# A hybrid of selective scan, convolution and spectral layers: one C multiply of twelve moves from GpSimd to VectorE, softplus's PSUM bank is counted as free one slot later, and one bias of three in the feed-forwards moves to VectorE

## The chip, the cores and the metric

The kernel runs on one core of a Trainium2 chip. The metric is the device time of one launch in microseconds, and lower is better. The engines are named as in the profile: PE is TensorE (matmuls; PEld are its weight loads), DVE is VectorE, ACT is ScalarE, POOL is GpSimd, SP is SyncE, whose queue issues all the DMAs here.

## The reference, cut to what matters

The input is x, four images of 96 channels and 64 by 64 pixels. Each goes through a group norm and four layers:

```python
# layer 0, a selective scan; K = 4 directions, DI = 192 channels, N = 16 states, L = 4096 pixels
u = silu(depthwise_conv3x3(Win @ x) + conv_b)
xs = [u, transposed u, reversed u, reversed transposed u]
dts_r, Bs, Cs = split(sel_w[k] @ xs[k])                  # 6, 16 and 16 rows
delta = softplus(dt_w[k] @ dts_r + dt_b)
for l in range(L):                                       # for each direction, channel d, state n
    h[d, n] = h[d, n] * exp(delta[d, l] * A[d, n]) + delta[d, l] * xs[d, l] * Bs[n, l]
    y[d, l] = sum_n h[d, n] * Cs[n, l]
y = layer_norm(sum of the four directions + Ds * xs); x = x + Wout @ y

# layer 1: 1x1 expansion to 576, depthwise 3x3, 1x1 back, with batch norms and relu
# layer 2: a spectral layer (FFT over the 4096 pixels, relu(X * r + b), inverse FFT), then a feed-forward
# layer 3: linear attention with 6 heads, then a feed-forward
# both feed-forwards, on layer-normed tokens, 96 -> 384 -> 96, with the rounding of fp8e5 and fp16:
h = relu(fp16(fp16(fp8(x) @ fp8(W1).T) + fp8(b1)))
y = fp16(fp16(fp8(h) @ fp8(W2).T) + fp8(b2))
```

## The kernel before, in words

**The scan.** The scan runs over 128 steps: 4 images, 4 directions each, 8 chunks of 512 pixels each. A step has 12 units; a unit is 64 channels (two halves `e` of 32) by 4 states, so 128 partitions by two times 512 elements. Four engines work on a unit, each in the order in which the instructions are written:

- GpSimd multiplies the step's delta times u (`rep_g`) with B (`rep_BC`): one product of 128x1024, `db`, in `inputs` (line 1206).
- ScalarE computes exp(delta times A) into a PSUM bank, `ps_da`, once for each half, in `decays` (line 1216). There are four such banks, which is two units.
- VectorE runs the recurrence with TENSOR_TENSOR_SCAN, once for each half, in `states` (line 1225).
- The result is multiplied with C. The units listed in `POOL_C` write the scan's result to SBUF (`hc`), and GpSimd multiplies both halves in one instruction, in `product` (line 1244). For the others the scan writes over `ps_da`, and VectorE multiplies each half into `hc` (line 1229).
- The last column of a unit's states is kept for the next chunk (`keep`): by GpSimd for the units of `POOL_C` (line 1241, one copy for both halves), by ScalarE for the others (line 1239, a copy for each half). The last chunk of a direction keeps nothing.
- PE sums over states and channels into the bank `ps_y`, for two units at a time, in `sums` (line 1265).

The scan is one loop over slots, one for each of the 1536 units. In slot s it writes out, in this order: the DMAs due; the state copies of unit s - 1 and the exponentials of unit s + 1; the C product of unit s - 1, if it is GpSimd's; the product db of unit s + 2; the scans of unit s; the sums of the pair that ended two slots ago. `db` and `hc` have three and five buffers.

**The work beside it.** All the rest (the inputs of the scan of later images, called fronts; the re-ordering of the directions, called turns; the convolutions; the spectral layers; layers 2 and 3) is cut into small portions on PE, ScalarE and VectorE, written as Python generators. A planner writes portions into each slot behind the scan's instructions. A portion states its engine, an assumed time, and the number of banks `mm` that it takes: `yield ac(0.65)` is one of 0.65 us on ScalarE. A slot has an allowance of 3.0 us on PE, 2.4 on ScalarE and 1.5 on VectorE. A stream's next portion on another engine is written in a later slot than the one before it, as a rule. There are three `mm` banks; `held_banks` counts those in use. `bank()` adds one where a matmul is written, and `free()` takes one off where the last reader of the bank is written, so that a matmul into that bank may be written in the same slot. At the start of each slot the count `freed` is taken off `held_banks` and set to zero:

```python
            tensor[0] = 0.0
            held_banks[0] -= freed[0]
            freed[0] = 0
```

Nothing adds to `freed` in the kernel before.

The stages come in the order of `plan`: weights, front 1, front 2, then for image 0 turn, convolution, spectral twice, layer 2, layer 3, then front 3, then the same for images 1 and 2, where layer 3 has the next image's turn beside it. The last image's convolution starts under the scan; when the scan is over (`alone` is filled then) the rest of it and layers 2 and 3 of the last image run without the planner.

**Softplus** (`scan_inputs`, lines 590 to 619) makes delta. A part is one matmul of the step sizes (lines 594, 598), three activations, Abs, Exp and Ln, on ScalarE (603, 605, 607), a maximum and addition on VectorE in the bank (609), the product with u (612), and a copy of the bank to SBUF on ScalarE (616). There are three parts for each of 16 chunk and direction pairs of an image. The last line of a part calls `free()`.

**The feed-forwards** (`feed_forward`) have three groups of 128 hidden rows, m = 0, 1, 2. Each is a matmul in fp8 (884), a copy to fp16 on ScalarE (887), bias and relu on ScalarE (895) or, in the part after the scan, on VectorE (892), and a conversion to fp8 (901, or 898 on VectorE for m = 1 after the scan).

Of the kernel before, what the change touches and what calls it, by code (L numbers as in the profile page):

```python
# [41 lines left out]
KORDER = [(0, 1, 3, 2)] * (B - 1) + [(1, 3, 0, 2)]  # L42

SCAN = {"rep_d": 3, "rep_g": 3, "rep_BC": 5, "db": 3, "hc": 5}
POOL_C = (1, 3, 5, 7, 9, 11)
TMP, IN = 10, 5

PC = NI * NJ // 2
# [46 lines left out]
def hybrid_kernel(ctx: ExitStack, tc: tile.TileContext, a: dict):  # L95
# [18 lines left out]
    alone = []  # L114
# [5 lines left out]
    def bank(tag="mm", turn=True):  # L120

        if alone and tag == "mm" and turn:
            tag = turns(alone)
        if tag == "mm":
            held_banks[0] += 1
        return psum.tile([128, CH], F32, name=f"ps_{tag}", tag=tag, bufs=BANKS[tag])

    held_banks, freed = [0], [0]

    def free(n=1):  # L130

        held_banks[0] -= n


    tc.keep_in_program_order(nc.scalar.preload_act_table_set("natural_log_exp_and_others"))
# [5 lines left out]
    def const(name, rows=slice(0, 128)):  # L141
        return cst[rows, CS[name]]

    def col(name, i=0, rows=slice(0, 128)):
        at = COL[name].start + i
        return cols[rows, at : at + 1]
# [40 lines left out]
    def tmp(name, shape=(128, CH), dtype=F32):  # L187

        if alone and dtype == F32:
            tag = turns(spare)  # L190
            if tag in SCAN:
                return pair(tag)[:, 0, : shape[1]]
        return bp.tile(list(shape), dtype, name=name, tag="tmp", bufs=TMP)
# [31 lines left out]
    def split(t):  # L225
        return t.rearrange("p (a b) -> p a b", a=RPC)

    def view(t, o, c):

        if o == 0:  # L230
            return split(t[:, chunk(c)])
        return t.rearrange("p (h w) -> p w h", h=H)[:, c * RPC : (c + 1) * RPC, :]
# [69 lines left out]
    def later_weights():  # L302
# [16 lines left out]
        yield dv(0.8)  # L319
        nc.vector.tensor_copy(wout_bias, p[:C, 0:1])  # L320
        free()
        nc.vector.tensor_scalar(wo_a, wo_a, col("lng_a"), None, ALU.mult)
        nc.vector.tensor_scalar(wo_b, wo_b, col("lng_b", rows=slice(0, 64)), None, ALU.mult)
# [104 lines left out]
    def later(out, t, then=None):  # L428

        to_store.append((out, t, then))  # L430
# [140 lines left out]
    def scan_inputs(b, u, o, c, done):  # L571

        i = b % 3
        if not done.issuperset([c] if o == 0 else range(NCH)):
            while not done.issuperset([c] if o == 0 else range(NCH)):
                yield wait(1)
            yield wait(2)
        ua, ub = u
        yield pe(1.8, 1)
        p = bank()  # L580
        mm(p, lhsT=sel[:, o, 0, :], rhs=view(ua, o, c), start=True, stop=False)
        mm(p, lhsT=sel[:, o, 1, :], rhs=view(ub, o, c), start=False, stop=True)

        yield ac(0.7)
        xd = tmp("xd")
        act(xd, p, AF.Identity, bias=col("one"))
        free()
        for e in (0, 1):
            later(d_bc[o + 2 * e][i][c], xd[64 * e : 64 * e + 2 * NS])
        for part in range(3):  # L590
            yield pe(0.9, 1, part > 0)
            p = bank()
            if part < 2:
                mm(p, lhsT=dtw[:, o + 2 * part, 0:128], rhs=xd, start=True, stop=True)  # L594
                at = [(slice(0, 128), o + 2 * part, slice(0, 128))]
            else:
                for e in (0, 1):
                    mm(p[64 * e : 64 * e + 64], lhsT=dtw[:, o + 2 * e, 128:DI], rhs=xd, start=True, stop=True)
                at = [(slice(64 * e, 64 * e + 64), o + 2 * e, slice(128, DI)) for e in (0, 1)]

            yield ac(0.65)
            z = tmp("z")
            act(z, p, AF.Abs)  # L603
            yield ac(0.65)
            act(z, z, AF.Exp, scale=-1.0)
            yield ac(0.65)
            act(z, z, AF.Ln, bias=1.0)  # L607
            yield dv(0.7)
            nc.vector.scalar_tensor_tensor(p, p, 0.0, z, ALU.max, ALU.add)  # L609
            yield dv(0.85)  # L610
            g = tmp("g")
            nc.vector.tensor_mul(split(g), split(p), view(ub if part == 2 else ua, o, c))
            for rows, k, ch in at:
                later(d_du[k][i][c][ch], g[rows])
            yield ac(0.6)
            nc.scalar.copy(z, p)  # L616
            free()
            for rows, k, ch in at:
                later(d_delta[k][i][c][ch], z[rows])
        traced[b].add((o, c))  # L620
# [232 lines left out]
    def layer_norm(x, out, rows=128):  # L853


        yield pe(0.9, 1)
        p = bank()
        mm(p, lhsT=const("cen", slice(0, x.shape[0])), rhs=x, start=True, stop=True)  # L858
        yield ac(0.7)
        r = tmp("r")  # L860
        act(r, p, AF.Square)
        yield pe(0.9, 1)
        v = bank()
        mm(v, lhsT=const("mean"), rhs=r, start=True, stop=True)  # L864
        yield ac(1.3)
        rsqrt(r, v)
        free()
        yield dv(0.85)
        if out.dtype == F8:
            nc.vector.tensor_tensor(out, r, p, ALU.mult, saturate=False)  # L870
        else:
            nc.vector.tensor_mul(out, split(r[:rows]), split(p[:rows]))
        free()

    def feed_forward(x, weights):

        wq1, wq2, bq = weights
        xq = tmp("xq", (128, CH), F8)
        yield from layer_norm(x[:C], xq)
        hq = tmp("hq", (128, 3, CH), F8)  # L880
        for m in range(3):
            yield pe(0.5, 1, m > 0)
            p = bank()
            mm(p, lhsT=wq1[:, m * 128 : (m + 1) * 128], rhs=xq, start=True, stop=True)
            yield ac(0.65)
            acc = tmp("acc16", (128, CH), F16)
            nc.scalar.copy(acc, p)  # L887
            free()
            if alone:

                yield dv(0.75)
                nc.vector.tensor_scalar(acc, acc, bq[:, m : m + 1], 0.0, ALU.add, ALU.max)
            else:
                yield ac(0.65)
                act(acc, acc, AF.Relu, bias=bq[:, m : m + 1])
            if alone and m == 1:
                yield dv(0.75)
                nc.vector.tensor_copy(hq[:, m, :], acc, saturate=False)
            else:
                yield ac(0.65)  # L900
                nc.scalar.activation(hq[:, m, :], acc, AF.Copy, saturate=False)  # L901
        yield pe(1.4, 1)
        p = bank()
        for m in range(3):
            mm(p[:C], lhsT=wq2[:, m, :], rhs=hq[:, m, :], start=m == 0, stop=m == 2)
        yield ac(0.65)
        acc = tmp("acc16", (128, CH), F16)
        nc.scalar.copy(acc[:C], p[:C])
        free()
        yield ac(0.65)  # L910
        act(acc[:C], acc[:C], AF.Identity, bias=bq[:C, 3:4])
        yield pe(1.4, 1)
        p = bank()
        mm(p[:C], lhsT=ident16, rhs=acc[:C], start=True, stop=False)
        mm(p[:C], lhsT=const("ident", slice(0, C))[:, :C], rhs=x[:C], start=False, stop=True)  # L915
        yield ac(0.65)
        nc.scalar.copy(x[:C], p[:C])
        free()
# [183 lines left out]
    def front(b):  # L1102


        u, there, done = [], set(), set()

        def memory():
            u.extend([big("ua")[:, :L], big("ub")[:, :L]])
            if b > 0:
                yield from normalised(b, arriving(b), there)  # L1110
                return

            chunks = [(c, fetch_image(b, c, tmp)) for c in range(NCH)]
            load(cst[:, CS["grp"]], a["cst"][:, CS["grp"]])
            load(cols, a["cols"])
            first_weights()
            yield from group_norm(b, chunks)
            yield from normalised(b, chunks, there)

        streams = [memory()]  # L1120
        for c in range(0, NCH, 2):
            streams.append(input_conv(b, u, c, there, done))
            for e in (c, c + 1):
                streams.append(scan_inputs(b, u, 0, e, done))
        streams += [scan_inputs(b, u, 1, c, done) for c in range(NCH)]
        return [Stage("front", 3 if b == 0 else 4, *streams)]
# [21 lines left out]
    def scans(stages):  # L1148
# [13 lines left out]
        for number, step in enumerate(steps):  # L1162
            step["at"] = number % (K * NCH)
            u = 0
            for which, chans in enumerate(PASSES):
                for j in range(NJ):
                    for i in chans:
                        units.append({"step": step, "number": number, "u": u, "j": j, "i": i, "pass": which,
                                      "pool": u in POOL_C})
                        u += 1  # L1170
# [402 lines left out]
```

## Time and profile before

| what | before |
|---|---|
| runs | 6701.09, 6704.47, 6705.06 us; median 6704.47 |
| profiled execution | 6709.47 us; span 6707.7 us, 84354 instructions |
| PE busy | 4872.1 us, 73% of the span |
| VectorE busy | 5391.2 us, 80% |
| ScalarE busy | 4269.2 us, 64% |
| GpSimd busy | 5488.7 us, 82% |
| granted TensorE clock, mean | 0.828 of full speed |
| HBM read and written | 881.28 and 239.01 MB, 167 GB/s over the span |

In a line of groups of the profile stand: line, engine, operation, output <- inputs (buffer numbers left out), shapes, count, then busy us and mean ns of one, then the idle time of the engine just before it and what ended most of that. A line of waits has the waiting instruction, the one that released it, the us in total, the number of times and the longest. A line of the timeline has start, us, and the instruction, with the idle time before it in brackets. In a table of stretches each engine's busy us is followed by its number of instructions.

### The profile page before, as it was taken

How to read it: one execution, taken by the hardware profiler on the slowest of the kernel's cores; microseconds unless marked ns; L12 is line 12 of the kernel's file. 1: busy time of each engine (PE TensorE's matmuls, PEld its weight loads, DVE VectorE, ACT ScalarE, POOL GpSimd, SP SyncE). 2: the span in 40 equal slices, each digit the busy share in tenths (PEclk: the TensorE clock that was granted, in tenths of full speed). 3: DMA queues.
4: the chain of work that ended last, by engine and by line, in shares of the span. 5: the costliest groups of instructions: out<-in, count | busy, mean ns of one | idle time of the engine just before them, and what ended most of it. 6: DMA issues, size and time to landing. Idle time of an engine off the chain costs nothing. (4 is left out here: it accounts for less than half of the span.)

```text
span 6707.7 us, 84354 instructions
## 1 busy us (share of the span) xinstructions
PE 4872.1 (73%) x27884; PEld 1775.4 (26%) x27884; DVE 5391.2 (80%) x5611; ACT 4269.2 (64%) x8008; POOL 5488.7 (82%) x2983
## 2 busy tenths in 40 slices
PE   7624767656987776775688877777887776859998
PEld 2101212111223521221122254211223521212383
DVE  5979888788989888888899887988988888888021
ACT  5744776654665677877466657866665676756356
POOL 4868778788999999977999988999999899899000
PEclk9756878768998887886799877878998877869998
DMA  5644555566544544455764445465644554554131
GB/s 189 197 150 144 183 189 181 174 218 219 184 148 143 199 158 147 155 186 188 246 214 146 143 160 167 157 219 186 188 147 146 189 161 161 200 180 156 35 94 38
DMA packets 438824, 1121.41 MB, mean 167 GB/s; under 512 B 73002, under 2 KB 74768, under 8 KB 437140
## 3 DMA queue, kind: packets, MB, share of 16 engines
q1 hardware_dynamic: 438388, 1116.02, 50.7%
q8 instruction: 222, 3.64, 0.2%
q14 instruction: 214, 1.75, 0.1%
HBM read 881.28 MB, written 239.01 MB: 167 GB/s over the span
## 5 line engine op out<-in xcount | busy, mean ns | idle before, releaser
L1206 POOL TENSOR_TENSOR db<-rep_g,rep_BC 128x1024 f32<-128x1024 f32 x1536 | 3602.0, 2365 | 194.1 <-DVE ps_da L1225 115.0
L1216 ACT ACTIVATE ps_da<-rep_d,aneg 128x512 f32<-128x512 f32 x3072 | 2053.5, 689 | 499.4 <-DVE hc L1225 381.7
L1225 DVE TENSOR_TENSOR_SCAN ps_da<-ps_da,state,db 128x512 f32<-128x512 f32 x1344 | 1722.9, 1282 | 371.8 <-ACT state L1239 226.7
L1244 POOL TENSOR_TENSOR hc<-hc,rep_BC 128x1024 f32<-128x1024 f32 x768 | 1813.4, 2361 | 131.8 <-DVE hc L1225 64.8
L1225 DVE TENSOR_TENSOR_SCAN hc<-ps_da,state,db 128x512 f32<-128x512 f32 x1344 | 1645.8, 1266 | 173.0 <-ACT ps_da L1216 155.9
L1265 PE MATMUL ps_y<-hc,cst 128*32 128x512 f32 x6144 | 1037.4, 755 | 781.5 <-POOL hc L1244 759.5
L1229 DVE TENSOR_TENSOR hc<-ps_da,rep_BC 128x512 f32<-128x512 f32 x1536 | 1062.3, 692 | 91.3 <-DVE ps_da L1225 1.3
L1265 PEld LDWEIGHTS ps_y<-hc,cst 128*32 128x32 f32 x6144 | 141.7, 119 | 1450.8 <-POOL hc L1244 1096.0
L1241 POOL COPY state<-hc 128x2 f32<-128x2 f32 x672 | 128.4, 191 | 395.3 <-DVE hc L1225 374.1
L1239 ACT COPY state<-ps_da 128x1 f32<-128x1 f32 x1344 | 212.8, 158 | 343.9 <-DVE hc L1229 343.0
L805 PE MATMUL ps_mm<-h,wd 128*32 128x512 f32 x3192 | 365.7, 593 | 7.7 <-ACT r L154 7.0
L543 PE MATMUL ps_mm<-xp,taps 128*128 128x512 f32 x576 | 299.3, 660 | 42.5 <-ACT xp L523 15.7
L1276 ACT COPY yt<-ps_y 128x512 f32<-128x512 f32 x256 | 149.9, 585 | 222.3 <-PE ps_y L1265 212.2
L594 PE MATMUL ps_mm<-xd,dtw 128*128 128x512 f32 x256 | 176.9, 785 | 156.9 <-ACT z L616 131.9
L782 PE MATMUL ps_mm<-wd,w 128*32 128x512 f32 x2128 | 271.4, 624 | 22.9 <-DMA wd<-x 12.8
L1225 DVE TENSOR_TENSOR_SCAN ps_da<-ps_da,db 128x512 f32<-128x512 f32 x192 | 234.6, 1222 | 56.9 <-ACT state L1239 36.0
L1225 DVE TENSOR_TENSOR_SCAN hc<-ps_da,db 128x512 f32<-128x512 f32 x192 | 223.4, 1204 | 17.3 <-ACT ps_da L1216 13.2
L603 ACT ACTIVATE z<-ps_mm 128x512 f32<-128x512 f32 x192 | 114.3, 596 | 189.1 <-PE ps_mm L594 112.4
L609 DVE SCALAR_TENSOR_TENSOR ps_mm<-ps_mm,z 128x512 f32<-128x512 f32 x192 | 131.9, 687 | 84.0 <-ACT z L607 56.4
L864 PE MATMUL ps_mm<-r,cst 128*128 128x512 f32 x210 | 144.9, 778 | 62.7 <-ACT r L154 17.4
L940 PE MATMUL ps_mm<-wa,xp 128*64 128x96 f32 x1728 | 133.3, 317 | 71.0 <-DVE d L944 62.3
L786 ACT ACTIVATE h<-ps_mm 128x512 f32<-128x512 f32 x266 | 153.9, 596 | 44.6 <-PE ps_mm L782 42.5
(418 smaller groups left out, 6879.9 us busy)
## 6 DMA issues: line engine op xcount, KB each, us to landing
rep_BC<-bc SPq DMA_DIRECT2D x512, 512.0 KB
rep_g<-du SPq DMA_DIRECT2D x384, 512.0 KB
rep_d<-delta SPq DMA_DIRECT2D x384, 512.0 KB
y<-yt SPq DMA_DIRECT2D x512, 128.0 KB
du<-g SPq DMA_DIRECT2D x128, 256.0 KB
delta<-z SPq DMA_DIRECT2D x128, 256.0 KB
tab<-in_etab SPq DMA_DIRECT2D x128, 256.0 KB
ypart<-y SPq DMA_DIRECT2D x72, 256.0 KB
```

Of the source, the lines that this page charges most:

```text
L543: mm(p, lhsT=taps[:, t, 0:128], rhs=window(t, c + e), start=t == 0, stop=t == 8)
L594: mm(p, lhsT=dtw[:, o + 2 * part, 0:128], rhs=xd, start=True, stop=True)
L782: mm(p[32 * n : 32 * n + 32], lhsT=w1[:, 32 * g : 32 * g + 32], rhs=xin[:, n : n + 15 : 2, 1 : W + 1], start=True, stop=True)
L786: act(h[:, :, 1 : W + 1], split(p), AF.Relu)
L805: mm(p[32 * n : 32 * n + 32], lhsT=held["wd"][:, groups[i], o, dx, :], rhs=here[i][:, :, dx : dx + W], start=dx == 0, stop=dx == 2)
L1206: nc.gpsimd.tensor_mul(x["db"], x["step"]["g"][x["i"]], both(x["step"]["BC"][x["j"]][:, 0]))
L1216: act(x["da"][e], x["step"]["d"][x["i"]][:, e], AF.Exp, scale=aneg[:, av : av + 1])
L1225: nc.vector.tensor_tensor_scan(x["h"][e][:, order], x["da"][e][:, order], x["db"][:, e, order], start, ALU.mult, ALU.add)
L1229: x["made"] = nc.vector.tensor_mul(x["hc"][:, e], x["h"][e], x["step"]["BC"][x["j"]][:, 1])
L1239: nc.scalar.copy(to[:, e : e + 1], x["h"][e][:, end : end + 1])
L1244: x["made"] = nc.gpsimd.tensor_mul(x["hc"], x["hc"], both(x["step"]["BC"][x["j"]][:, 1]))
L1265: done = mm(y[32 * q : 32 * q + 32], lhsT=const("stack"), rhs=x["hc"][:, e], start=first or (x["pass"] == 0 and x["j"] == 0), stop=last or ...
```

## The change

`POOL_C` has five entries instead of six: units 1, 3, 6, 8 and 10 of each twelve have their C product on GpSimd; before it was every odd unit. `free` gets a parameter: with `behind=True` it adds one to `freed`, so that the bank counts as held until the next slot begins. Softplus's last line uses it. In the feed-forwards the group m = 1 takes the VectorE form of bias and relu under the scan too; its conversion to fp8 there stays on ScalarE.

```diff
-POOL_C = (1, 3, 5, 7, 9, 11)
+POOL_C = (1, 3, 6, 8, 10)
...
-    def free(n=1):
-
-        held_banks[0] -= n
+    def free(behind=False):
+
+        (freed if behind else held_banks)[0] += 1 if behind else -1
...
             nc.scalar.copy(z, p)
-            free()
+            free(behind=True)
...
             nc.scalar.copy(acc, p)
             free()
-            if alone:
+            if alone or m == 1:
 
                 yield dv(0.75)
                 nc.vector.tensor_scalar(acc, acc, bq[:, m : m + 1], 0.0, ALU.add, ALU.max)
```

## The prediction

> **What bounds the kernel now.** I read the busy shares first, then cut the span into its stages (a table of busy time by stretch), then the timeline of a quiet stage, then the waits. A measurement of this kernel tells about 0.2% (13 us) from no change.
>
> ```profile
> PE 4872.1 (73%) x27884; PEld 1775.4 (26%) x27884; DVE 5391.2 (80%) x5611; ACT 4269.2 (64%) x8008; POOL 5488.7 (82%) x2983
> ```
>
> Over the whole span no engine is full: GpSimd (POOL) 82%, VectorE (DVE) 80%. By stage it is different. Columns: us, busy us of PE, weight loads, VectorE, ScalarE, GpSimd, then clock and DMA.
>
> ```profile
> core 0: us, PE busy (x) PEld busy (x) DVE busy (x) ACT busy (x) POOL busy (x), PEclk, DMA share, GB/s
> ...
> 628.00:1445.00 817.00, 559.85 (x1664) 156.20 (x1664) 686.81 (x722) 568.94 (x1048) 630.19 (x341) 0.78 0.56 182
> ...
> 1445.00:1625.00 180.00, 117.18 (x298) 24.82 (x299) 139.23 (x136) 74.21 (x154) 161.84 (x92) 0.75 0.66 224
> ...
> 1625.00:2097.00 472.00, 395.36 (x2277) 110.11 (x2275) 427.78 (x434) 299.14 (x586) 464.25 (x255) 0.93 0.52 169
> ...
> 2097.00:2345.00 248.00, 185.77 (x2657) 142.34 (x2657) 223.53 (x228) 154.29 (x274) 225.81 (x122) 0.84 0.54 181
> ...
> 2345.00:2600.00 255.00, 179.20 (x808) 64.72 (x806) 225.51 (x233) 204.25 (x391) 246.40 (x134) 0.83 0.47 154
> ...
> 5890.00:6203.00 313.00, 224.36 (x1133) 63.73 (x1130) 274.62 (x274) 179.35 (x351) 304.45 (x167) 0.82 0.50 162
> ...
> 6203.00:6707.70 504.70, 444.23 (x4060) 252.33 (x4058) 82.24 (x161) 266.80 (x418) 2.37 (x1) 0.94 0.19 56
> ```
>
> In order: the two fronts, a turn, a convolution, a spectral stage, a layer 2, the last image's convolution under the scan, and the tail after the scan. In the convolution GpSimd is busy 464.25 of 472 us (98%), VectorE 91%. In layer 2 GpSimd has 97%, in the fronts only 77% with VectorE at 84%. GpSimd has nothing in the tail. The groups behind it:
>
> ```profile
> L1206 POOL TENSOR_TENSOR db<-rep_g,rep_BC 128x1024 f32<-128x1024 f32 x1536 | 3602.0, 2365 | 194.1 <-DVE ps_da L1225 115.0
> ...
> L1244 POOL TENSOR_TENSOR hc<-hc,rep_BC 128x1024 f32<-128x1024 f32 x768 | 1813.4, 2361 | 131.8 <-DVE hc L1225 64.8
> ...
> L1229 DVE TENSOR_TENSOR hc<-ps_da,rep_BC 128x512 f32<-128x512 f32 x1536 | 1062.3, 692 | 91.3 <-DVE ps_da L1225 1.3
> ```
>
> The timeline of a layer 3 shows one period of GpSimd:
>
> ```profile
> 2603.47 1.29 DVE L1225 TENSOR_TENSOR_SCAN ps_da<-ps_da,state,db 128x512 f32<-128x512 f32 x1 [0.54 <-POOL db L1206]
> ...
> 2607.38 0.24 DVE L1058 TENSOR_TENSOR vk<-vk,ps_mm 96x96 f32<-96x96 f32 x1
> ...
> 2608.25 4.67 POOL L1206 TENSOR_TENSOR db<-rep_g,rep_BC 128x1024 f32<-128x1024 f32 x2
> ...
> 2608.33 2.44 DVE L1225 TENSOR_TENSOR_SCAN hc<-ps_da,state,db 128x512 f32<-128x512 f32 x2
> ...
> 2612.88 0.18 POOL L1241 COPY state<-hc 128x2 f32<-128x2 f32 x1
> ...
> 2613.13 2.35 POOL L1244 TENSOR_TENSOR hc<-hc,rep_BC 128x1024 f32<-128x1024 f32 x1
> ...
> 2615.44 4.66 POOL L1206 TENSOR_TENSOR db<-rep_g,rep_BC 128x1024 f32<-128x1024 f32 x2
> ```
>
> From 2608.25 to 2615.44 (7.19 us for two units) GpSimd runs without a gap: two db products (4.67), state copy and C product (2.56). VectorE's unit with C on GpSimd takes 2.45 us; the other kind runs from 2603.47 to 2607.38, 3.91 us with both multiplies. Together 6.36, so VectorE waits 0.8 us. A step of 12 units takes 6 x 7.19 = 43.1 us: **GpSimd bounds these stages.** The fronts are bound otherwise:
>
> ```profile
> DVE ps_da L1225 <- ACT state L1239: 57.8, 22, 7.7
> ACT z L603 <- PE ps_mm L594: 63.9, 37, 5.1
> ```
>
> There ScalarE stands still for a matmul that waits for a bank (second line), and VectorE waits for ScalarE (first line).
>
> **What the Trainium skill says.** "Perfetto Trace Analysis", section Identifying the Most-Contended Engine, takes occupancy as the measure for VectorE, ScalarE and GpSimd, and (Optimization Strategy) warns that the most contended engine changes between regimes; the table above is just that. "SBUF — State Buffer", section Who interferes with whom: a VectorE instruction with at most one SBUF input outside the two-port modes never meets GpSimd; tensor_scalar can enter such a mode, and then, as with two SBUF inputs, the one that starts second is blocked for the other's whole instruction. The moved C multiply reads one PSUM and one SBUF operand: free of it, and the trace agrees (692 ns beside a busy GpSimd). The moved bias is a 16-bit tensor_scalar in SBUF. The trace has it only in the tail; for the block it has the two-SBUF-input addition of line 952, under the scan and in the tail:
>
> ```profile
> L952 DVE TENSOR_TENSOR d<-d,rib x12: 337/2032/2509, 2110.8 to 5258.3; 1x96 f32<-1x96 f32 x12
> ...
> L952 DVE TENSOR_TENSOR d<-d,rib x4: 344/348/358, 6374.6 to 6445.7; 1x96 f32<-1x96 f32 x4
> ...
> L892 DVE TENSOR_SCALAR acc<-acc,bq x48: 343/348/354, 6527.0 to 6696.7; 128x512 f16<-128x512 f16 x48
> ```
>
> With GpSimd busy its 12 calls sum to 18.37 us, 1.53 each, against 0.35: a wait of 1.18 us, never above one GpSimd product. "VectorE: DVE Perf Modes", section The perf-mode tier table, gives tensor_scalar on 16-bit SBUF data four elements a cycle; 348 ns for 512 elements (0.68 ns each, overhead included) fits that.
>
> **The change, part by part.**
>
> *C multiplies.* One unit of twelve moves, 128 in all. GpSimd loses 2.56 us each (328 us). VectorE gains 3.91 - 2.45 = 1.46 each (187 us). ScalarE gets 2 x 112 state copies of 158 ns (35 us). No DMA and no load moves. The new order (1, 3, 6, 8, 10) has neighbours 4, 5 and 11, 0 both on VectorE; a product at an even unit also ends a slot earlier against the sums that wait for it, so PE queues less behind it.
>
> *Bias.* 48 of m = 1 under the scan (6 stages of 8 chunks; those of the tail are on VectorE already). ScalarE loses 48 x 0.721 = 35 us, which cancels the copies. VectorE gets 48 x 1.53 = 73 us; ends 48 x 0.35 = 17 and 48 x 2.7 = 130. I take 1.53, since GpSimd is over 90% busy there too. Queued behind it on VectorE: the next scan, for which ScalarE's exponentials and GpSimd's next db wait. The chain of the chunk also gets two more engine changes, so slots; three chunks run side by side.
>
> *Bank.* No instruction is added. The planner counts the bank of each softplus part as held one slot longer, so the next matmul goes out when the copy is done instead of standing on PE in front of it. It costs slots: a front has 48 parts, each holding one of 3 banks some 4 slots. Following the planner's rules through the code (slots, no times), the two fronts take 185 slots instead of 178, the third 91 instead of 88, and a layer 3 a few less, as ScalarE's allowance was its limit. (For the kernel before the count has the first product of the first turn in slot 300; in the trace it starts at 1478.20 us, when some 300 db products have been started.) The stores of du and delta move with their parts on SP's queue, by a slot, past loads of the scan; the scan of images 1 to 3 needs them a hundred slots later and more, and image 0's front ends at slot 71 in place of 74. The last convolution enters at slot 1450 of 1536 in both, and what is left of it at the end is the same, because it waits for scan outputs. So I cost the **tail at nothing**: 504.7 us as before; without that cover each slot lost there is some 2 us of PE.
>
> By stage, with slots from the db products' busy time over 2.345 us (1536 in sum):
> - Convolutions of images 0 to 2: 1407 us, 391 slots (32.6 steps), VectorE 1278, GpSimd 1390. After: VectorE 1278 + 48 = 1326, GpSimd 1390 - 83 = 1307. VectorE is late next. With 2% of waits 1353: **-54** (-75 if nothing waits, -20 if the pattern is not evened out).
> - Last convolution under the scan: 313 us, 85 slots: VectorE 275 + 10 = 285, GpSimd 286; with 4.5% waits 299: **-14** (-20 to 0).
> - Layers 2 and 3 without a turn: 950 us, 257 slots: VectorE 836 + 31 + 32 x 1.53 = 916, GpSimd 861. ScalarE is 80% busy, so 3.5% of waits: 949, **0** (-30 to +35).
> - Turns, with the layer 3 beside two of them: 945 us, 239 slots: VectorE 761 + 29 + 24 = 814, GpSimd 805. PE's long products hold ScalarE there: **-8** (-35 to +25).
> - Spectral: 743 us, 182 slots: VectorE 642 + 22 = 664: **-3** (-20 to +20).
> - Fronts 1 to 3: 1217 us, 265 slots: VectorE +32 if its waits stay. ScalarE's waits for the softplus matmuls are 155 us; if half go and half of that reaches VectorE, -39. Together **-5** (-50 to +32).
> - Start to 628 us, 117 slots: +14 on VectorE, much of it in waits: **+4** (-5 to +14).
>
> Sum -80. The profiled execution took 6709.47 us (span 6707.7), the median of the runs is 6704.47, 5 us (0.07%) lower; I take the sum from the median: **6624 us**.
>
> **Rivals.**
> 1. *VectorE becomes the bound everywhere (slower).* Outside the convolutions VectorE gets 187 - 58 = 129 us of multiplies and 73 of biases. Its waits there are mostly for ScalarE, not GpSimd, so they may stay and the 202 show. With 70 of gain in the convolutions it decides from 70/202, a third, showing; at half, +31: 6735. For it: VectorE at 84 to 88% in these stages; the port wait. Against: GpSimd was 91 to 97% busy in turns and layers 2 and 3 and is relieved by 2.56 a step.
> 2. *The new order is lumpy.* Units 6 to 11 need 3 x 2.56 + 6 x 2.34 = 21.7 us of GpSimd against 19.1 of VectorE; units 0 to 5 20.5 of VectorE against 19.2. If the three db buffers carry nothing over, a step costs 21.7 + 20.5 = 42.2 in place of 40.9: 1.3 us more in the 40 steps of the convolutions, total 6676. Against: the lag to be carried is only 21.7 - 19.1 = 2.6 us, and db runs two units ahead.
> 3. *The bank pays in full.* Two thirds of the 155 us reach VectorE (-71 in the fronts in place of -5) and the bias waits little (-18): 6540. Against: part of these waits is the matmul itself, 1 to 2 us at the clock granted there.
> 4. *Nothing of it shows:* the bank is rarely the limit and GpSimd's relief ends in VectorE's load: within 13 us of 6704.
>
> **How the numbers follow.** The forecast, with rival 2 within its own range of 6560 to 6691, 0.55; rival 3 0.15; no difference 0.11; rival 1 0.19. Faster by over 0.2%: 0.70; within: 0.11; slower: 0.19. The range takes half of rival 3 and a third of rival 1: 6530 to 6740.
>
> **What would show it.** In the convolutions GpSimd falls to about 96% and VectorE rises to 97 or 98%, a step takes 41 to 42 us, and VectorE no longer waits for db. Line 892 under the scan has a median above 1 us; at 0.35 the port step was wrong. ScalarE's wait at line 603 falls below 100 us over the fronts. The tail stays at 500 to 510 us; if it grew, the slot count was wrong. A convolution still at 43 us a step, or VectorE under 90% there, would make the main step wrong.

## The result, and the profile after

The kernel after takes 6617.73 us (median of four runs, 6606.63 to 6625.16) against 6702.78 us for the kernel before on the same chip: a ratio of 0.9869, 95% interval 0.9858 to 0.9881. The forecast was 6624. The profiled execution has a span of 6616.0 us, 91.7 us less than before. Where the time came from is not where the forecast put most of it.

The page's busy shares after:

```profile
PE 4823.8 (73%) x27884; PEld 1774.2 (27%) x27884; DVE 5593.1 (85%) x5915; ACT 4284.8 (65%) x8184; POOL 5183.8 (78%) x2743
```

GpSimd has fallen from 82% to 78% and VectorE has risen from 80% to 85%, as intended. The table of stretches after, cut at the events that begin a stage (two fronts, a turn, a convolution, a spectral stage, a layer 2, the last image's convolution under the scan, the tail); columns as in the prediction:

```profile
core 0: us, PE busy (x) PEld busy (x) DVE busy (x) ACT busy (x) POOL busy (x), PEclk, DMA share, GB/s
...
634.00:1413.00 779.00, 547.13 (x1696) 152.48 (x1696) 725.13 (x774) 586.50 (x1095) 618.25 (x326) 0.81 0.60 195
1413.00:1588.00 175.00, 120.56 (x312) 25.64 (x312) 149.52 (x149) 80.68 (x172) 158.29 (x87) 0.78 0.67 232
1588.00:2048.00 460.00, 394.79 (x2276) 110.92 (x2278) 443.02 (x462) 301.59 (x600) 445.13 (x236) 0.91 0.54 175
2048.00:2328.00 280.00, 209.63 (x2832) 161.28 (x2829) 243.10 (x249) 170.54 (x313) 226.04 (x121) 0.81 0.52 172
2328.00:2581.00 253.00, 167.98 (x652) 53.56 (x652) 235.16 (x249) 189.64 (x371) 225.11 (x119) 0.79 0.45 149
...
5798.00:6124.00 326.00, 237.81 (x1246) 67.58 (x1250) 293.42 (x301) 188.03 (x376) 292.63 (x156) 0.83 0.51 163
6124.00:6616.00 492.00, 431.07 (x3954) 247.10 (x3946) 77.43 (x155) 262.15 (x411) 0.00 (x0) 0.94 0.19 56
```

In the convolution (460 us) GpSimd is busy 97% and VectorE 96%. In the fronts VectorE has gone from 84% of the time to 93%: 817.00 - 686.81 = 130 us of idle time in the prediction's stretch have become 779.00 - 725.13 = 54. In layer 2 VectorE now has 93% and GpSimd 89%.

The same stages in all kernels can be compared through slots, one for each of the 1536 units; the slots of a stretch are the busy time of its db products (line 1206) over 2.345 us. In each cell: us, slots, us per slot.

| stage | before | C alone | bank alone | bias alone | after |
|---|---|---|---|---|---|
| start | 629, 116.7 | 647, 117.5 | 631, 114.3 | 629, 116.7 | 634, 114.6 |
| fronts 1 to 3 | 1212, 263.1, **4.607** | 1220, 262.7, 4.644 | 1138, 273.5, **4.161** | 1211, 261.9, 4.623 | 1165, 275.0, **4.237** |
| turns, with the layer 3 beside | 851, 213.5, 3.985 | 858, 214.9, 3.993 | 889, 221.0, 4.022 | 893, 224.0, 3.987 | 867, 216.1, 4.013 |
| convolutions 0 to 2 | 1433, 397.7, **3.603** | 1385, 399.1, **3.470** | 1435, 397.9, 3.606 | 1430, 396.6, 3.606 | 1394, 401.3, **3.473** |
| spectral | 819, 203.5, 4.024 | 829, 201.2, 4.121 | 831, 205.4, 4.046 | 835, 206.0, 4.053 | 827, 201.3, 4.108 |
| layers 2 and 3 | 938, 253.8, 3.695 | 957, 253.5, 3.776 | 911, 243.3, 3.745 | 912, 243.4, 3.746 | 911, 241.2, 3.777 |
| last convolution | 333, 87.6, 3.801 | 329, 86.9, 3.788 | 307, 80.0, 3.835 | 333, 87.9, 3.787 | 326, 86.2, 3.780 |
| tail | 492.7 | 491.8 | 492.5 | 491.9 | 492.0 |

After against before, each stage's change in us per slot times its slots after: fronts -102, convolutions -52, last convolution -2, layers 2 and 3 +20, spectral +17, turns +6; start +5, tail -1. That is -109; the other +17 are slots that moved from cheap stages to the fronts, which take 275 in place of 263, priced at what a slot cost before. Sum -92.

The groups of the page after that answer to those shown of before:

```profile
L1206 POOL TENSOR_TENSOR db<-rep_g,rep_BC 128x1024 f32<-128x1024 f32 x1536 | 3601.3, 2365 | 465.0 <-DVE ps_da L1225 349.7
...
L1244 POOL TENSOR_TENSOR hc<-hc,rep_BC 128x1024 f32<-128x1024 f32 x640 | 1512.1, 2363 | 112.8 <-DVE hc L1225 58.7
...
L1229 DVE TENSOR_TENSOR hc<-ps_da,rep_BC 128x512 f32<-128x512 f32 x1792 | 1239.2, 692 | 109.7 <-PE ps_y L1265 1.4
```

A product costs what it cost (2365 and 692 ns). What has changed is the idle time ahead of db: 465.0 us in place of 194.1, of which 349.7 wait for a scan on VectorE. GpSimd has handed over 301 us of products (1813.4 - 1512.1) and now waits for the engine that took them. The waits in fronts 1 and 2 after (waiting instruction, releaser, us, times, longest):

```profile
DVE ps_da L1225 <- ACT state L1239: 15.1, 11, 3.0
...
ACT z L603 <- PE ps_mm L594: 24.4, 18, 5.1
```

VectorE's wait for ScalarE's state copy was 57.8 us there and is 15.1; ScalarE's wait at line 603 for the matmul of line 594 was 63.9 and is 24.4.

### The profile page after: what moved, and what is told of

Its sections match the earlier page's. It is cut to its first block, busy times and chain, and to the rows that moved or that the text cites. A ratio compares the mean times of both kernels' runs of the same rounds, so it can differ in the third digit from the quotient of the medians.

```text
span 6616.0 us, 84626 instructions
## 1 busy us (share of the span) xinstructions
PE 4823.8 (73%) x27884; PEld 1774.2 (27%) x27884; DVE 5593.1 (85%) x5915; ACT 4284.8 (65%) x8184; POOL 5183.8 (78%) x2743
## 5 line engine op out<-in xcount | busy, mean ns | idle before, releaser
L1206 POOL TENSOR_TENSOR db<-rep_g,rep_BC 128x1024 f32<-128x1024 f32 x1536 | 3601.3, 2365 | 465.0 <-DVE ps_da L1225 349.7
L1225 DVE TENSOR_TENSOR_SCAN ps_da<-ps_da,state,db 128x512 f32<-128x512 f32 x1568 | 2005.7, 1279 | 211.6 <-ACT state L1239 156.4
L1244 POOL TENSOR_TENSOR hc<-hc,rep_BC 128x1024 f32<-128x1024 f32 x640 | 1512.1, 2363 | 112.8 <-DVE hc L1225 58.7
L1225 DVE TENSOR_TENSOR_SCAN hc<-ps_da,state,db 128x512 f32<-128x512 f32 x1120 | 1371.3, 1266 | 75.5 <-ACT ps_da L1216 49.5
L1229 DVE TENSOR_TENSOR hc<-ps_da,rep_BC 128x512 f32<-128x512 f32 x1792 | 1239.2, 692 | 109.7 <-PE ps_y L1265 1.4
L1239 ACT COPY state<-ps_da 128x1 f32<-128x1 f32 x1568 | 247.7, 158 | 526.1 <-DVE hc L1229 522.3
L1241 POOL COPY state<-hc 128x2 f32<-128x2 f32 x560 | 106.7, 190 | 352.7 <-DVE hc L1225 336.0
L1225 DVE TENSOR_TENSOR_SCAN ps_da<-ps_da,db 128x512 f32<-128x512 f32 x224 | 273.1, 1219 | 41.5 <-ACT state L1239 27.8
L1225 DVE TENSOR_TENSOR_SCAN hc<-ps_da,db 128x512 f32<-128x512 f32 x160 | 186.0, 1203 | 4.6 <-ACT ps_da L1216 4.6
L543 PEld LDWEIGHTS ps_mm<-xp,taps 128*128 128x128 f32 x576 | 116.7, 210 | 233.1 <-issue 162.9
L805 PEld LDWEIGHTS ps_mm<-h,wd 128*32 128x32 f32 x3192 | 104.2, 109 | 253.1 <-issue 211.7
```

The source lines that it names most:

```text
L543: mm(p, lhsT=taps[:, t, 0:128], rhs=window(t, c + e), start=t == 0, stop=t == 8)
L805: mm(p[32 * n : 32 * n + 32], lhsT=held["wd"][:, groups[i], o, dx, :], rhs=here[i][:, :, dx : dx + W], start=dx == 0, stop=dx == 2)
L1206: nc.gpsimd.tensor_mul(x["db"], x["step"]["g"][x["i"]], both(x["step"]["BC"][x["j"]][:, 0]))
L1225: nc.vector.tensor_tensor_scan(x["h"][e][:, order], x["da"][e][:, order], x["db"][:, e, order], start, ALU.mult, ALU.add)
L1229: x["made"] = nc.vector.tensor_mul(x["hc"][:, e], x["h"][e], x["step"]["BC"][x["j"]][:, 1])
L1239: nc.scalar.copy(to[:, e : e + 1], x["h"][e][:, end : end + 1])
```

## The experiments

Twelve kernels, each timed against the kernel before on the same chip. "C" is the number of units of twelve whose C product is on GpSimd.

| kernel | C | bank | m = 1 under the scan | us | ratio | 95% interval |
|---|---|---|---|---|---|---|
| c_only | 5 | | ScalarE | 6708.67 | 1.0006 | 0.9999 to 1.0012 |
| bank_only | 6 | yes | ScalarE | 6636.58 | 0.9901 | 0.9887 to 0.9914 |
| bias_only | 6 | | bias on VectorE | 6730.42 | 1.0041 | 1.0028 to 1.0053 |
| no_bias | 5 | yes | ScalarE | 6631.51 | 0.9895 | 0.9881 to 0.9908 |
| again (the whole change) | 5 | yes | bias on VectorE | 6615.75 | 0.9873 | 0.9858 to 0.9888 |
| no_c | 6 | yes | bias on VectorE | 6610.82 | 0.9864 | 0.9847 to 0.9880 |
| adapt | 5 in convolutions, else 6 | yes | ScalarE | 6598.32 | 0.9845 | 0.9830 to 0.9860 |
| copy_psum | 5 | yes | copy on VectorE | 6608.20 | 0.9861 | 0.9846 to 0.9876 |
| before_pause | 6 | | ScalarE | 6765.04 | 1.0096 | 1.0080 to 1.0111 |
| bias_pause | 6 | | bias on VectorE | 6739.86 | 1.0058 | 1.0045 to 1.0071 |
| bank_pause | 6 | yes | ScalarE | 6608.77 | 0.9861 | 0.9848 to 0.9875 |
| adapt_copy | 5 in convolutions, else 6 | yes | copy on VectorE | 6564.36 | 0.9796 | 0.9783 to 0.9809 |

### One part at a time

My theory was that of the prediction: C gives most of the gain. The rivals: VectorE's new load takes it back outside the convolutions, and the bank pays in full.

**c_only** has the first hunk of the diff alone.

```diff
-POOL_C = (1, 3, 5, 7, 9, 11)
+POOL_C = (1, 3, 6, 8, 10)
```

> Only the C multiplies move (five of twelve on GpSimd); bank and bias as before. Theory A (each part works in its own stages): the convolutions go from 3.60 to about 3.47 us per slot (-50 us), but the fronts, where VectorE and not GpSimd is short, get slower by up to 0.12 us per slot (+30), and turns, spectral and layers 2 and 3 gain or lose little. Total -10 to -40 us, 6663 to 6693. Theory B (GpSimd's relief alone also empties the waits of the fronts, the bank does nothing): fronts at 4.2 to 4.3 us per slot, total -80 to -95, 6608 to 6623.

It gives nothing: 1.0006, outside both forecasts. The stage table shows why. The planner does not read `POOL_C`, so the layers' parts stay in their slots and this comparison is clean stage by stage. The convolutions gain 48 us as forecast, and the rest loses 58: start 18, layers 2 and 3 19, spectral 10, fronts 8, turns 7, less 4 in the last convolution. The first convolution's waits of VectorE for db, before:

```profile
DVE ps_da L1225 <- POOL db L1206: 29.9, 43, 1.1
```

and with C alone:

```profile
DVE ps_da L1225 <- POOL db L1206: 0.2, 1, 0.2
```

That wait is gone (29.9 us to 0.2). Over the whole span of the same kernel, though, the db group reads

```profile
L1206 POOL TENSOR_TENSOR db<-rep_g,rep_BC 128x1024 f32<-128x1024 f32 x1536 | 3601.3, 2364 | 511.2 <-DVE ps_da L1225 413.7
```

A db buffer is free when the scan of its unit, here the one that writes `ps_da`, has read it. GpSimd's wait for that has gone from 115.0 us to 413.7. Outside the convolutions GpSimd's relief becomes waiting time, while of the 129 us of new work on VectorE there (128 x 1.46, less the 48 and 10 us in the convolutions) 62 us show, 48%: the 58 without the last convolution's 4. C also gives ScalarE 224 more state copies, about 35 us; no run separates these from the multiplies.

In the first layer 2 VectorE's largest wait is for ScalarE's state copy. Before:

```profile
DVE ps_da L1225 <- ACT state L1239: 7.4, 8, 2.4
```

and with C alone:

```profile
DVE ps_da L1225 <- ACT state L1239: 9.8, 6, 2.3
```

ScalarE's copies and exponentials there wait for VectorE in turn, 17.8 us before and 24.8 with C alone.

**bank_only** has `free(behind=True)` and its count alone.

```diff
-            free()
+            free(behind=True)
```

> Only softplus's bank is counted as held one slot longer; C multiplies and bias as before. Theory A: ScalarE's wait at line 603 falls from 189 us to below 80, the fronts fall from 4.61 to about 4.2 us per slot over some 270 slots (-80 to -110), every other stage stays (convolutions 3.60 us per slot). Total 6595 to 6625. Theory B: no more than 13 us from 6703, fronts at 4.6 us per slot.

Most of the gain of the change: 0.9901. But 6636.58 us is 12 above the upper end of theory A: the other stages were to stay, and turns, spectral stages and layers 2 and 3 cost 25 us more at equal slots. Its fronts 1 and 2 in the table of stretches:

```profile
631.00:1392.00 761.00, 550.89 (x1696) 152.96 (x1696) 701.95 (x741) 578.73 (x1066) 655.11 (x354) 0.81 0.61 198
```

VectorE is busy 92% there, with 59 us idle. The fronts' slot costs 4.161 us in place of 4.607, so -122 us over 273.5 slots; since the fronts also take ten slots more, the stage itself is 74 us shorter. That the same work is spread over more slots explains little of it: in fronts 1 and 2 VectorE's busy time fell from 3.90 to 3.84 us a slot, its idle time from 0.74 to 0.32. Of ScalarE's waits at line 603, over the whole span, the kernel before has

```profile
ACT z L603 <- PE ps_mm L594: 112.4, 70, 5.1
...
ACT z L603 <- PE ps_mm L598: 75.0, 48, 4.7
```

and with the bank alone

```profile
ACT z L603 <- PE ps_mm L594: 53.0, 41, 3.9
...
ACT z L603 <- PE ps_mm L598: 28.1, 19, 6.1
```

From 187.4 to 81.1 us. In fronts 1 and 2 the weight load of that matmul waits for the copy of line 616, which frees the bank, before

```profile
PEld ps_mm L594 <- ACT z L616: 122.6, 38, 7.7
```

and with the bank alone

```profile
PEld ps_mm L594 <- ACT z L616: 50.2, 21, 5.4
```

So the matmul stands less on PE in front of a bank that is not free.

**bias_only** has the last hunk alone, and **no_bias** all the others.

```diff
-            if alone:
+            if alone or m == 1:
```

> Only the bias of m = 1 moves to VectorE under the scan. Theory A: line 892 takes about 1.1 to 1.5 us under the scan as GpSimd is busier there than in the changed kernel, 50 to 70 us of VectorE in all; layers 2 and 3 have 12% of VectorE idle before, so part is hidden: total 0 to +25, 6703 to 6728, with fewer slots in the layer 3 stages. Rival (the port wait lies under VectorE's waits for db anyway, and ScalarE's 35 us count): -10 to -25.

> The changed kernel with the bias of m = 1 back on ScalarE (C multiplies and bank as changed). Theory A: layers 2 and 3 fall from 3.78 us per slot to 3.55 to 3.65, all else as in the changed kernel: 6585 to 6610. Rival (the slower layers 2 and 3 come from the C multiplies on VectorE, not from the port): within 8 us of 6618.

The bias alone costs 26 us, just above its range. C and bank together give what the bank gives, within the intervals, and miss both forecasts: layers 2 and 3 stay at 3.76 us a slot with the bias back on ScalarE, so the bias is not what makes them slow in the whole change. But the whole change is faster than the two together, so the bias seemed to gain there what it loses alone. That needed a second set.

### Does the bias gain beside the bank?

**again** is the kernel after once more; **no_c** is it with `POOL_C` as before.

> The whole change once more, beside the others of this call and against the same runs of the kernel before. C and bank together gave 0.9895 and the whole change 0.9869 in its first comparison; the bias alone cost 26 us (1.0041). If the bias truly gains beside the other two parts, this run gives 0.986 to 0.988 (about 6615 us). If the difference was between the comparisons, it gives 0.989 to 0.991.

> Bank and bias, with C on GpSimd in six units of twelve as before. Theory (the bias only adds load to VectorE, and what it gave the whole change is due to GpSimd being relieved): bank alone 0.9901 plus the bias's 26 us, 0.994 or about 6662. Rival (the bias relieves ScalarE, which the bank's gain leaves more exposed, whatever GpSimd does): 0.987 to 0.990, 6620 to 6638.

The first comparison of the whole change is confirmed (0.9873). And no_c went with its rival and a little past it: 0.9864, as fast as the whole change or a little faster. So C gives nothing beside the other two parts either (at equal slots its -54 us in the convolutions are paid with +23 in the fronts, +22 in the spectral stages and the rest in small change), and the bias, which costs 26 us alone, gains 26 beside the bank.

### Is it the place in the slots?

The bias exchanges a ScalarE portion for a VectorE one, and the bank holds portions back: both move the layers' parts against the scan's loads and sums. To see what such a move is worth with no instruction changed, three kernels get a pause of six slots in the planner:

```diff
             owed = min(owed + rate, 8.0)
+            if slot == 480:
+                owed -= 6 * rate
```

> The kernel before with one thing added: at slot 480 of 1536 the planner owes nothing for six slots, so that every later step of the layers lies six slots (half a step of the scan) later against the scan. No instruction is added or removed. This is for the bias, which cost 26 us alone (6730) and gained about 25 us beside the bank (6637 to 6611). Theory (where the layers' parts fall against the scan's loads and sums is worth some 25 us by itself, and the kernel before has a favourable place): 10 to 30 us slower, 1.0015 to 1.0045. Rival (the place is worth nothing, and the bias and the bank act on each other through an engine): within 0.15% of before.

> The bias alone, with the same pause of six slots at slot 480. Theory (place): away from the 6730 of the bias alone by 10 us or more, either way, likely towards 6704 to 6720 since few places can be as good as that of the kernel before. Rival (engine): 6730 again, within 8 us.

> The bank alone, with the same pause at slot 480, which leaves the fronts of images 1 and 2 and the first convolution untouched. Theory (place): away from the 6637 of the bank alone by 10 us or more, likely towards 6611, as the bank's layers lie in an unfavourable place that the bias happened to mend. Rival (engine): 6637 again, within 8 us. By both the fronts stay at 4.16 us a slot.

The place is worth more than I expected. The kernel before loses 63 us by the pause (twice the upper end of what the theory gave); the bank alone gains 28 and takes 6609, where the theory had 6611; the bias alone goes to 6740, with overlapping intervals, so its direction was missed and its size is not resolved. The bias thus costs 26 us on the kernel before and gains 25 on the same kernel with the pause. Its sign is one of place, and a reading of these 25 us as an engine's relief falls. The bank gains at both places, 67 us without the pause and 156 with it (6765.04 to 6608.77): its sign does not hang on the place, its size does. Stretches up to the pause are alike in the two kernels without the change; spectral stage 0 and layer 2 of image 0 with the pause:

```profile
2104.00:2401.00 297.00, 212.01 (x2857) 158.67 (x2858) 254.21 (x255) 177.76 (x316) 259.28 (x140) 0.81 0.51 168
2401.00:2655.00 254.00, 167.35 (x653) 52.31 (x654) 222.20 (x232) 192.78 (x372) 241.38 (x131) 0.79 0.46 151
```

The spectral stage takes 297 us where the kernel before has 267 by the same cut; 24 of these 30 are six slots at some 4 us, the pause itself, which the later stages need not lose, since the slots are 1536 in all. Layer 2 right behind it takes 254 us in place of 257. The loss sits later and in the rates (the profiled executions are 46 us apart, less than the medians): turns at 4.093 us a slot in place of 3.985 (23 us), spectral stages at 4.068 in place of 4.024 (9), layers 2 and 3 at 3.728 in place of 3.695 (8), spread over many waits of which none stands out. Which rule makes a place good stays open.

Two rates hardly depend on the place. In the kernels without the bank (five) a slot of the fronts costs 4.599 to 4.644 us, in those with the bank and six of twelve there 4.154 to 4.194 (five), with the bank and five of twelve 4.237 to 4.256. In the convolutions it is 3.600 to 3.612 with six of twelve and 3.466 to 3.498 with five. The fronts of images 1 and 2 lie ahead of the pause and of the first bias, so all kernels with the bank have them at the same place. The test is front 3, whose place differs: 4.52 to 4.58 us a slot without the bank, 4.15 to 4.25 with the bank and six of twelve.

### Each part where it pays

**adapt** keeps five of twelve to the steps of the convolutions.

```diff
-POOL_C = (1, 3, 6, 8, 10)
+POOL_C = (1, 3, 5, 7, 9, 11)
+POOL_CONV = (1, 3, 6, 8, 10)
+CONV = (*range(29, 40), *range(67, 77), *range(94, 105), *range(121, 127))
...
-                                      "pool": u in POOL_C})
+                                      "pool": u in (POOL_CONV if number in CONV else POOL_C)})
```

> Bank, bias on ScalarE, and five of twelve on GpSimd only in the steps of the four convolutions (29 to 39, 67 to 76, 94 to 104, 121 to 126), six elsewhere. Theory (the moved multiply gains some 50 us in the convolutions and gives them back in fronts, layers 2 and 3, spectral stages and the start): bank alone 6636 less 40 to 50, so 6585 to 6600, 0.982 to 0.985; the convolutions at 3.47 us a slot, the fronts at 4.16. Rival (what the convolutions gain is lost later whatever the split is, because the stages wait for each other): 6625 to 6640.

6598.32 us, 38 less than the bank alone; the stage table has the convolutions at 1395 us in place of 1435, and fronts (1137 and 1138) and layers 2 and 3 (911 and 911) as with the bank alone. The theory holds, and the place has no part in it, since the planner does not read the split: the C multiply's loss belongs to the stages outside the convolutions, and goes when the split there stays at six.

**copy_psum** is the kernel after, with another piece of m = 1 on VectorE:

```diff
-            yield ac(0.65)
+            yield dv(0.75) if m == 1 and not alone else ac(0.65)
             acc = tmp("acc16", (128, CH), F16)
-            nc.scalar.copy(acc, p)
+            if m == 1 and not alone:
+                nc.vector.tensor_copy(acc, p)
+            else:
+                nc.scalar.copy(acc, p)
             free()
-            if alone or m == 1:
+            if alone:
```

> As the whole change, but of the middle third (m = 1) VectorE takes the copy out of PSUM to 16 bits (line 887) and ScalarE keeps bias and Relu: one SBUF operand at most, so no wait for GpSimd. Theory (the moved bias costs 1.12 us in place of 0.35 because it waits for GpSimd's instruction to end): the copy takes 0.6 to 0.75 us each under the scan, with no end tied to GpSimd's, and the 48 of them save VectorE about 20 us; time 5 to 20 us below the whole change. Rival (1.12 us comes from something else, such as waiting on its own operands): about 1.1 us again and the same time as the whole change.

This tests why the moved bias is slow. The biases under the scan in the kernel after (count: shortest, median and longest ns, then from when to when):

```profile
L892 DVE TENSOR_SCALAR acc<-acc,bq x48: 322/1106/2541, 2353.2 to 5780.2; 128x512 f16<-128x512 f16 x48
```

and in copy_psum the copies under the scan, and the biases of its tail:

```profile
L888 DVE CAST acc<-ps_mm x48: 661/666/690, 2355.9 to 5799.4; 128x512 f16<-128x512 f32 x48
...
L895 DVE TENSOR_SCALAR acc<-acc,bq x48: 342/348/354, 6421.6 to 6591.6; 128x512 f16<-128x512 f16 x48
```

Alone, the bias takes 348 ns. Under the scan its median is three times that, and the longest is about one GpSimd product longer. The copy reads the same 128x512 elements from PSUM at twice the price of an undisturbed bias, but never meets anything: 661 to 690 ns in all 48. That agrees with "SBUF — State Buffer", section Who interferes with whom, for both forms. The timeline of a layer 3 after shows one wait:

```profile
2604.48 2.35 POOL L1206 TENSOR_TENSOR db<-rep_g,rep_BC 128x1024 f32<-128x1024 f32 x1 [0.59 <-DVE ps_da L1225]
...
2605.04 1.93 DVE L892 TENSOR_SCALAR acc<-acc,bq 128x512 f16<-128x512 f16 x1
...
2606.90 2.45 DVE L1225 TENSOR_TENSOR_SCAN hc<-ps_da,state,db 128x512 f32<-128x512 f32 x2
...
2609.27 0.32 DVE L892 TENSOR_SCALAR acc<-acc,bq 128x512 f16<-128x512 f16 x1
2609.41 0.23 POOL L1241 COPY state<-hc 128x2 f32<-128x2 f32 x1 [2.58 <-DVE hc L1225]
```

Line 892 starts at 2605.04, in the middle of a db product that ends at 2604.48 + 2.35 = 2606.83, and ends at 2606.97, 0.14 us after it. The next one starts at 2609.27 with GpSimd idle and takes 0.32 us. All 48 in the kernel after go one way or the other: 37 end 0.146 to 0.153 us after the end of a GpSimd instruction, whether they took 0.35 us or 2.54, and the other 11 take 0.32 to 0.35 us. The ratio of copy_psum, 0.9861, overlaps that of the whole change (0.9873), and the slots moved too; the duration is shown, a gain in time is not.

**adapt_copy** puts the two together.

> What did best, together: the bank, five of twelve on GpSimd in the convolutions' steps only, and of the middle third VectorE takes the copy out of PSUM in place of the bias. Theory (the three act in different stages and add up): five of twelve only in the convolutions gave 6598 beside 6637 for the bank alone, the bias beside the bank 25 us, the copy in its place 8 more: 6565 to 6575, 0.980 to 0.981. Rival (what the bias gave beside the bank was its place in the scan, which the new split shifts again): 6590 to 6605, as with the bias on ScalarE.

6564.36 us, where the theory had 6565 to 6575: 0.9796, the fastest of all kernels here, 53 us below the whole change. By the runs above, some of it may be its place in the slots.

## Why the prediction was right

The time was right by more than its steps were. The prediction had -80 us; the medians show -85 and the profile -92, made of other terms. That these sum to nearly the same is luck, the more so as a shift by six slots alone moved kernels of this set by -28 to +63 us.

- **Convolutions: right.** -54 forecast, -52 found at equal slots. A step takes 12 x 3.473 = 41.7 us (41 to 42 said; rival 2 had 42.2, so little of the lumpiness shows). GpSimd at 97% and VectorE at 96%, and the wait for db gone, were said too, VectorE one or two points higher.
- **The C multiply elsewhere: the step failed.** The terms for the start, layers 2 and 3, turns and spectral stages came to -7 us (4 + 0 - 8 - 3), the bias included, because GpSimd is relieved where it was 91 to 97% busy. C alone costs 54 us there (18 + 19 + 7 + 10): rival 1's mechanism, with 48% of the multiplies showing outside the convolutions where a third was to decide. GpSimd's occupancy was read as a bound in layers 2 and 3 too, but VectorE there waits for ScalarE, before and with C alone (the lines at c_only), and ScalarE's copies and exponentials for VectorE, and what VectorE is given lengthens that loop; that it is this loop is argued from the waits, not shown by a run of its own. This goes against a plain use of "Perfetto Trace Analysis", Identifying the Most-Contended Engine: in layers 2 and 3 the engine of highest occupancy got 5% less work (C alone: 3.560 to 3.375 us a slot) and the slot went from 3.695 to 3.776 us.
- **Fronts: right in kind, wrong in size.** -5 forecast, -102 found. The term was "if half go and half of that reaches VectorE, -39": with the bank alone it measures -122 over all three fronts, where 155 us of waits had been taken as its source. Both halves were too small: two thirds of the waits at line 603 after its two matmuls went in fronts 1 and 2 (63.9 + 40.6 us to 25.0 + 11.2), and VectorE's idle time there fell by as much as ScalarE's waits did (from 130 us to 59, and 68). This is rival 3's mechanism, at about its two thirds in fronts 1 and 2 (71 of 104.5 us reach VectorE). The cost of C beside it was right: +32 said, +23 found (from no_c to again).
- **Slots of the bank: right.** Ten more in the fronts by the planner's rules, and in the trace with the bank alone (273.5 - 263.1); twelve in the whole change (275.0), most of them taken from layers 2 and 3 (253.8 to 241.2), where the prediction had a few. The bias alone also takes ten slots from these layers (243.4). The **tail cost nothing**: 492.7 us before, 492.0 after, by the same cut at the scan's end.
- **Bias: right mechanism, size too large.** 1.53 us each was taken from line 952; line 892 measures 54.0/48 = 1.12 under the scan. (Its 348 ns alone were read as fitting four elements a cycle; one length does not tell the rate from the fixed cost, so no run here shows that.) Its effect on the time, 26 us either way, was not in any step: it is one of place.
- **Last convolution: -14 said, -2 found.** VectorE's waits there are not for db alone.

So the sum stood because two errors had opposite signs: the fronts were 97 us better than said, and the stages other than fronts and convolutions of images 0 to 2 came to +45 (20 + 17 + 6 - 2 + 5 - 1) where -21 was said; the 17 us of slots moved into the fronts were not in the sum at all. Rival 1 was true of the C multiply, rival 3 of the bank.

## What to carry to other kernels

Where work moves between two engines, price it stage by stage, and where the stages differ let the split differ: the same multiply gained some 50 us in the convolutions and lost some 60 in the other stages, and confined to the convolutions it gave 38. A portion that holds a scarce PSUM bank is worth a look before any engine's load, since one count of a bank gained 67 us by itself and neither piece of moved arithmetic gained anything by itself. And where a planner places work in slots, a single part's time carries tens of us of place: judge it by the rate of the stage that it touches, or by the same part at another place.

## What the runs showed of the hardware that was not expected

A six-slot shift of the planned work with no instruction changed moved this kernel by +63 us, and the one with the bank by -28, of about 6700. And a 16-bit tensor_scalar in SBUF, 348 ns alone, took 322 to 2541 ns beside a busy GpSimd, while a copy from PSUM to 16 bits of the same shape took 661 to 690: beside a busy GpSimd the slower form is the faster one.
